# A decoder layer on one core: in the slots of the self attention, scores by keys are issued ahead of scores by queries

## The chip, the cores and the metric

The kernel runs on one core of a Trainium2 chip. Its engines are TensorE (PE in the profile, with PEld for its weight loads), VectorE (DVE), ScalarE (ACT), GpSimd (POOL) and SyncE (SP, which here only issues DMA transfers). The metric is the device time of one execution in microseconds (us). Before the change the median of three runs is 703.72 us (701.57 to 704.51).

## The reference

One decoder layer on x of shape (4, 1024, 256), four batches, in float32:

```
x = x + self_attention(layernorm(x))            # windows of 128, 16 heads of 16
x = x + cross_attention(layernorm(x), context)  # 77 keys, a mask, projections with biases
x = x + ffn(layernorm(x))                       # fake-quantised, silu(gate) * up, 704 wide
```

In the self attention a query of chunk c sees the keys of chunk c-1 and, causally, those of its own chunk c:

```
scores = einsum('bhcqd,bhckd->bhcqk', qc, kcat) / HD ** 0.5
scores = where(causal & valid, scores, -inf)
out    = einsum('bhcqk,bhckd->bhcqd', softmax(scores), vcat) @ w_out
```

## The kernel before, in words

The attention phase is a software pipeline written out by hand: the order of the instructions on each engine is the order in which the Python code issues them. Its work is cut into jobs, self attention (S) or cross attention (X) of one batch, in the order S0, S1, S2, X0, S3, X1, X2, X3. A job is cut into groups (g, o) of four heads, and a group into units u: four units of two 128-row tiles for S, two units of four tiles for X. That makes 96 units, and one slot of the main loop (line 1120) for each, after some slots ahead of the first.

Scores are computed twice. By queries (`sc_n`, `maxima`, line 616, products at L627) they stand with queries on the partitions, and VectorE takes each row's maximum from them (L657, with the causal mask `cboth` added); by keys (`sc_t`, `weights`, line 701, products at L712) they stand with keys on the partitions, and ScalarE takes the exponentials (L722), GpSimd zeroes what is not causal (L726). For the second kind, the negated maxima must already stand in `q`: each head has 16 spare rows there, and one of them, against a row of ones in `k`, adds the maximum's negative to every product. `put_maxima` (line 676) brings them there: a transpose on TensorE (`ps_mx`, L679), a copy on ScalarE (`mxT`, L683) and four DMA transfers issued by SyncE (L686). So `sc_t` of a group's first unit waits for these transfers, and `sc_n` of a unit runs LEAD = 5 slots ahead of its `sc_t`.

In slot number `slot` the loop handles `now`, the unit of this number, and `ahead`, the unit five later. A slot issues in this order: weighted values (`ps_av`, L756) with their transpose on VectorE (L780) and the normalising (L788, L790, L802) for units two slots back, in every second slot; tasks chosen by due times and costs, which are projections (`project`, L583, emptied by ScalarE), values (`values`, L564, emptied by ScalarE), transposes of normed rows (`normed_T`, L544), output projections (`out_project`, L811, added to x by VectorE at L820), and preparation of weights, mask and cross keys; work beside them on VectorE (statistics at L189, quantising of the FFN's weights at L426 to L436); `put_maxima` if a group is complete; then the block that the change touches, the scores of `ahead` and of `now`.

All products of this phase go to one pool of eight PSUM banks (`ps_b`, line 204), handed out in the order of the program. A tile waits until the tile eight places earlier has been read to the end. A slot takes four banks for `sc_n`, four for `sc_t`, and one or two for each task. `max_bias` and `weight_bias` only take the banks for S units; for X units they also issue a product with the mask.

[...]

Of the kernel before, what the change touches and what calls it, by code (L numbers as in the profile page):

```python
# [24 lines left out]
def decoder_layer(  # L25
# [33 lines left out]
    B, S, D = x.shape  # L59
# [139 lines left out]
    with ExitStack() as att:  # L199
# [6 lines left out]
        def bank(name):  # L206
            return ps_b.tile([P, 512], F32, name=name, tag="b")
# [393 lines left out]
        def max_bias(job, g, o, u):  # L601

            if u == 0:
                job.mx[g, o] = work.tile([P, NJ, NT], F32, name="mx", tag="mx", bufs=3)
            job.nb = banks = [bank("sc_n") for _ in range(NJ)]
            for j in range(NJ):
                if job.kind == "X":
                    nc.tensor.matmul(  # L608
                        banks[j][:, : HT * SK],
                        ident_bf,  # L610
                        mb_n[:, u * HT : (u + 1) * HT, :].rearrange("p t k -> p (t k)"),
                        start=True,
                        stop=False,
                    )
# [61 lines left out]
        def put_maxima(job, g, o):  # L676

            ps = bank("ps_mx")
            nc.tensor.transpose(  # L679
                ps[: NJ * NT, :P], job.mx[g, o].rearrange("p j t -> p (j t)"), ident  # L680
            )
            mxT = work.tile([NJ * NT, P], F32, name="mxT", tag="mxT", bufs=2)
            nc.scalar.copy(mxT, ps[: NJ * NT, :P])  # L683
            for j in range(NJ):
                row = j * SL + (1 - o) * HD
                nc.sync.dma_start(  # L686
                    out=job.q[g, o][row : row + 1, :],
                    in_=mxT[j * NT : (j + 1) * NT, :],
                )

        def weight_bias(job, g, o, u):

            job.tb = banks = [bank("sc_t") for _ in range(NJ)]
            if job.kind == "X":
                s = slice(u * HS, (u + 1) * HS)
                for j in range(NJ):
                    nc.tensor.matmul(  # L697
                        banks[j][:SK], ident_bf[:SK, :SK], mb_t[:, s], start=True, stop=False
                    )

        def weights(job, g, o, u):

            q, banks = job.q[g, o], job.tb
            if job.kind == "S":
                k = job.k[g, o]
                w = 0
                for i in range(2):
                    t = 2 * u + i
                    n = min(2 * P, S - t * P)
                    for j in range(NJ):  # L710
                        r = slice(j * SL, (j + 1) * SL)
                        nc.tensor.matmul(  # L712
                            banks[j][:, w : w + n],
                            k[r, t * P : (t + 1) * P],
                            q[r, t * P : t * P + n],
                            start=True,
                            stop=True,
                        )
                    w += n
                for j in range(NJ):  # L720
                    pt = work.tile([P, 2, 2, P], F32, name="pt", tag="pt", bufs=16)
                    nc.scalar.activation(  # L722
                        pt.rearrange("p i a q -> p (i a q)")[:, :w], banks[j][:, :w], AF.Exp
                    )

                    nc.gpsimd.affine_select(  # L726
                        out=pt[:, :, 0, :],
                        in_=pt[:, :, 0, :],
                        compare_op=ALU.is_ge,
                        fill=0.0,  # L730
                        base=0,
                        pattern=[[0, 2], [1, P]],
                        channel_multiplier=-1,
                    )
                    job.pts[g, o, j, u] = pt
            else:
                k = kx[:, g, o, job.b * SK : (job.b + 1) * SK]
                s = slice(u * HS, (u + 1) * HS)
                for j in range(NJ):
                    r = slice(j * SL, (j + 1) * SL)  # L740
                    nc.tensor.matmul(banks[j][:SK], k[r, :], q[r, s], start=False, stop=True)  # L741
                for j in range(NJ):
                    pt = work.tile([SK, HS], F32, name="ptx", tag="pt", bufs=16)
                    nc.scalar.activation(pt, banks[j][:SK], AF.Exp)  # L744
                    job.pts[g, o, j, u] = pt
# [36 lines left out]
        def normalise(job, g, o, hf, tail):  # L782

            if o == 0:
                job.aN[g, hf] = work.tile([P, HS], F32, name="aN", tag="aN", bufs=2)
            on = job.av[g, o, hf].rearrange("p (s e) -> p s e", e=SL)
            rec = small.tile([P, HS // SL, 1], F32, name="rec")
            nc.vector.reciprocal(rec, on[:, :, HD : HD + 1])  # L788
            aN = job.aN[g, hf].rearrange("p (s e) -> p s e", e=SL)
            (nc.gpsimd if tail else nc.vector).tensor_tensor(  # L790
                aN[:, :, o * HD : (o + 1) * HD],
                on[:, :, 0:HD],
                rec.to_broadcast([P, HS // SL, HD]),
                ALU.mult,
            )

        def by_features(job, g, o, hf):

            if o == NS - 1:
                if g == 0:  # L800
                    job.aT[hf] = work.tile([P, NC, HS], F32, name="aT", tag="aT", bufs=3)
                nc.vector.transpose(job.aT[hf][:, g, :], job.aN[g, hf])  # L802
# [317 lines left out]
        for slot in range(first, last):  # L1120
            present["slot"] = slot
            now = units[slot] if 0 <= slot < N else None
            ahead = units[slot + LEAD] if 0 <= slot + LEAD < N else None
            for fn, args in early.get(slot, ()):
                fn(*args)
            tail = slot >= N - LEAD
            if slot == N:

                pair = values_of[slot] + values_of.pop(slot + 1)
                for args in pair:  # L1130
                    weighted_values(*args)
                    normalise(*args, tail)
                for args in pair:
                    by_features(*args)
                while beside:
                    t = min(beside, key=lambda t: t[1:3])
                    beside.remove(t)
                    t[4](*t[5])
                    while after:
                        after.pop(0)()  # L1140
                last_project(jobs[-1])
            else:
                for args in values_of.get(slot, ()):
                    weighted_values(*args)
                    normalise(*args, tail)
                    if not tail:
                        by_features(*args)
            spent = 0.0
            cap = 1.35 if now and ahead else 2.3
            while t := next_in(tasks, slot, spent, cap):  # L1150
                spent += t[3]
                fn, args = t[4:]
                fn(*args)
                if fn is out_project:
                    job, hf, t2 = args
                    if job.kind == "X" and t2 == HT // 2 - 1:
                        third_norm(job.b, hf, slot)
            spent = 0.0
            while t := next_in(beside, slot, spent, 1.2):
                spent += t[3]  # L1160
                t[4](*t[5])
            if tail and slot < N:
                for args in values_of.get(slot, ()):
                    by_features(*args)
            for args in puts.get(slot, ()):
                put_maxima(*args)
            if ahead:
                max_bias(*ahead)
                if now and now[0].kind == "X":
                    weight_bias(*now)  # L1170
                maxima(*ahead)
            if now:
                if not (ahead and now[0].kind == "X"):
                    weight_bias(*now)
                weights(*now)
            for fn, args in late.get(slot, ()):
                fn(*args)
            while after:
                after.pop(0)()
# [6 lines left out]
    with ExitStack() as ffn:  # L1186
# [237 lines left out]
        ahead = []  # L1424
# [57 lines left out]
```

## Time and profile before

| what | value |
|---|---|
| median of three runs | 703.72 us |
| the profiled execution, its own time | 704.22 us |
| its span | 702.5 us |
| mean granted TensorE clock | 0.99 |
| TensorE busy | 654.3 us (93%) |
| VectorE busy | 546.7 us (78%) |
| ScalarE busy | 367.5 us (52%) |
| GpSimd busy | 268.5 us (38%) |
| first `sc_t` of slot 0 | 38.8 us |
| slots 0 to 42 (`now` and `ahead` both S) | 36.4 to about 269 us |
| slots 56 to 66 (both S again) | 349.9 to about 407 us |

A profile row of the kind "L657 DVE ... x512 | 172.7, 403 | 39.4 <-PE sc_n L627 38.9" gives the line, engine and operation, the count, the busy time, the mean duration in ns, and behind the last bar the idle time of that engine just before these instructions with what ended most of it. Ends of matmuls are modelled, so a busy TensorE is not a TensorE at its peak. In a row of waits the numbers are the total in us, the count and the longest.

### The profile page before, as it was taken

To read this page: it belongs to the slowest core of one execution; us is meant where nothing else is said; L and a number is where in the kernel's file an instruction comes from. 1 tells how busy PE (TensorE), PEld (TensorE's weight loads), DVE (VectorE), ACT (ScalarE), POOL (GpSimd) and SP (SyncE) were. 2 spreads that over 40 slices of the span, in tenths; PEclk is the share of its full clock that TensorE was granted. 3 is DMA by queue.
4 is the path that set the end of the run, shared out by engine and by line. 5 is a ranking of instruction groups with operands and counts; after the bars stand their busy time and mean duration, and the time that the engine had idled before them with its cause. 6 is when DMAs were issued, how large, how long until landed. Compare 5 with 4: busy or idle time off the path is not lost.

```text
span 702.5 us, 17376 instructions
## 1 busy us (share of the span) xinstructions
PE 654.3 (93%) x6465; PEld 404.3 (58%) x6470; DVE 546.7 (78%) x1917; ACT 367.5 (52%) x672; POOL 268.5 (38%) x517
## 2 busy tenths in 40 slices
PE   8989999999999889999999999999999999778776
PEld 5566566667665666655567666544554537334555
DVE  5688769669787798667879977766766868789987
ACT  3545555534656436534464465345445475498393
POOL 4055524536236386700064787234411024111022
PEclk9999999999999999999999999999999999999999
DMA  8000100000000000000000000000000000000048
GB/s 291 9 3 11 35 3 18 2 19 19 24 4 9 10 10 11 20 2 17 3 9 25 26 24 24 3 2 4 17 17 3 18 17 16 0 2 0 1 67 174
DMA packets 18645, 17.02 MB, mean 24 GB/s; under 512 B 3788, under 2 KB 18049, under 8 KB 18561
## 3 DMA queue, kind: packets, MB, share of 16 engines
q1 hardware_dynamic: 16369, 14.08, 6.4%
q0 software_dynamic: 1904, 1.84, 2.1%
q8 instruction: 51, 0.84, 0.5%
q14 instruction: 33, 0.27, 0.1%
q10 hardware_dynamic: 288, 0.00, 0.0%
HBM read 9.35 MB, written 6.03 MB: 22 GB/s over the span
## 4 chain that ended last, share of the span: by engine, by line
PE 70%; DVE 17%; ACT 6%; issue 4%; DMA 1%; POOL 1%; SPq 0%; ACTq 0%; DVEq 0%
PE ps_p L583 12%; PE sc_n L627 8%; PE ps_av L756 8%; PE sc_t L712 8%; PE ps_op L811 7%; PE sc_n L642 4%; PE ps_av L766 4%; PE sc_t L741 3%; PE ps_v L564 3%; PE sc_t L697 3%; DVE junk L657 2%; PE ps_t L544 2%; DVE bnst L189 2%; PE sc_n L608 2%; DVE hq L1391 1%
## 5 line engine op out<-in xcount | busy, mean ns | idle before, releaser
L657 DVE CUSTOM_DVE_ANT_0 junk<-sc_n,cboth 128x256 bf16<-128x256 f32 (+1 forms) x512 | 172.7, 403 | 39.4 <-PE sc_n L627 38.9
L722 ACT ACTIVATE pt<-sc_t 128x512 f32<-128x512 f32 (+1 forms) x256 | 125.4, 576 | 99.1 <-PE sc_t L712 96.6
L726 POOL TENSOR_SCALAR_AFFINE_SELECT pt<-pt 128x256 f32<-128x256 f32 x256 | 102.3, 408 | 117.4 <-ACT pt L722 107.2
L744 ACT ACTIVATE ptx<-sc_t 77x512 f32<-77x512 f32 x128 | 65.5, 592 | 77.3 <-PE sc_t L741 77.3
L712 PE MATMUL sc_t<-q,k 32*128 32x256 f32 (+1 forms) x1024 | 87.9, 380 | 2.8 <-DMA q<-mxT 1.4
L668 DVE TENSOR_REDUCE mx<-sc_n 128x4 f32<-128x308 f32 x128 | 52.2, 470 | 37.0 <-PE sc_n L642 36.9
L627 PE MATMUL sc_n<-k,q 32*128 32x256 f32 (+1 forms) x1024 | 79.7, 391 | 0.7 <-DVE mx L657 0.7
L157 POOL TENSOR_SCALAR ve<-mv 128x4 f32<-128x4 f32 x20 | 4.6, 232 | 196.9 <-DVE mv L191 196.8
L712 PEld LDWEIGHTS sc_t<-q,k 32*128 32x128 f32 x1024 | 66.8, 188 | 13.4 <-ACT q L597 2.3
L529 POOL TENSOR_SCALAR xn<-x,mv,rs 128x256 f32<-128x256 f32 x56 | 70.2, 1260 | 0.0
L627 PEld LDWEIGHTS sc_n<-k,q 32*128 32x128 f32 x1024 | 49.6, 185 | 30.0 <-DVE mx L657 10.7
L583 PE MATMUL ps_p<-xnT,w_s 128*128 128x512 f32 x128 | 61.8, 611 | 2.5 <-DVE mx L657 1.1
L780 DVE STREAM_TRANSPOSE o_sb<-ps_av 128x512 f32<-128x512 f32 x63 | 45.0, 714 | 23.6 <-PE ps_av L756 14.4
L756 PE MATMUL ps_av<-pt,vt 128*32 128x256 f32 (+1 forms) x1152 | 59.2, 349 | 2.4 <-DVE mx L657 2.3
L756 PEld LDWEIGHTS ps_av<-pt,vt 128*32 128x32 f32 x1152 | 34.8, 110 | 30.7 <-DVE mx L657 6.0
L657 DVE DVE_READ_ACCUMULATOR2_ANT mx<- 128x1 f32 x512 | 42.6, 83 | 0.0
L642 PEld LDWEIGHTS sc_n<-kx,q 32*128 32x128 f32 x1024 | 31.5, 186 | 14.5 <-issue 14.5
L697 PE MATMUL sc_t<-mb_t,ident_bf 77*77 77x512 bf16 x128 | 35.3, 379 | 4.0 <-ACT q L593 3.6
L583 PEld LDWEIGHTS ps_p<-xnT,w_s 128*128 128x128 f32 x128 | 22.2, 189 | 28.1 <-issue 17.1
L642 PE MATMUL sc_n<-kx,q 32*128 32x77 f32 x1024 | 36.2, 277 | 0.0
L766 PE MATMUL ps_av<-ptx,vx 77*32 77x512 f32 x256 | 35.2, 604 | 0.6 <-DVE mx L668 0.6
L1304 DVE SCALAR_TENSOR_TENSOR hT<-pu,usc,act 128x512 f32<-128x512 f32 x44 | 30.6, 744 | 6.4 <-ACT act L1303 6.1
(204 smaller groups left out, 1097.7 us busy)
## 6 DMA issues: line engine op xcount, KB each, us to landing
x<-in_x_dram SPq DMA_DIRECT2D x8, 512.0 KB
out_dram<-y SPq DMA_DIRECT2D x9, 256.0 KB
q<-mxT SPq DMA_DIRECT2D x128, 4.0 KB
out_dram<-x SPq DMA_DIRECT2D x7, 256.0 KB
out_dram<-y POOLq DMA_DIRECT2D x7, 256.0 KB, 4.7
w_s<-in_L_attn_w_qkv_dram SPq DMA_DIRECT2D x2, 384.0 KB
raw_d<-in_L_ffn_w_down_dram SPq DMA_DIRECT2D x2, 352.0 KB
raw_f<-in_L_ffn_w_gate_dram SPq DMA_DIRECT2D x5, 128.0 KB
```

Of the source, the lines that this page charges most:

```text
L529: eng.tensor_scalar(xn, xb[job.b][:, t, :], job.st[hf].mv[:, i, 0:1], job.st[hf].rs[:, i : i + 1], ALU.subtract, ALU.mult,)
L583: nc.tensor.matmul(ps, w[:, c, g * P : (g + 1) * P], job.xnT[hf][:, c, :], start=(c == 0), stop=(c == NC - 1),)
L627: nc.tensor.matmul(banks[j][:, (i + 1) * 2 * P - n : (i + 1) * 2 * P], q[r, t * P : (t + 1) * P], k[r, k0 * P : k0 * P + n], start=True, s ...
L642: nc.tensor.matmul(banks[j][:, i * SK : (i + 1) * SK], q[r, t * P : (t + 1) * P], k[r, :], start=False, stop=(i == HT - 1),)
L657: nc.vector.tensor_tensor_reduce(out=junk[:, 2 * P - n :], in0=banks[j][:, (i + 1) * 2 * P - n : (i + 1) * 2 * P], in1=cboth[:, 2 * P - n ...
L697: nc.tensor.matmul(banks[j][:SK], ident_bf[:SK, :SK], mb_t[:, s], start=True, stop=False)
L712: nc.tensor.matmul(banks[j][:, w : w + n], k[r, t * P : (t + 1) * P], q[r, t * P : t * P + n], start=True, stop=True,)
L722: nc.scalar.activation(pt.rearrange("p i a q -> p (i a q)")[:, :w], banks[j][:, :w], AF.Exp)
L726: nc.gpsimd.affine_select(out=pt[:, :, 0, :], in_=pt[:, :, 0, :], compare_op=ALU.is_ge, fill=0.0, base=0, pattern=[[0, 2], [1, P]], channe ...
L744: nc.scalar.activation(pt, banks[j][:SK], AF.Exp)
L756: nc.tensor.matmul(ps[j * SL : (j + 1) * SL, (a0 - t0) * P : (a1 - t0) * P], slot_of(job.vs[kb // 2][:, kb % 2], heads[j]), job.pts[g, o, ...
L766: nc.tensor.matmul(ps[j * SL : (j + 1) * SL, :], slot_of(vx[:, job.b], heads[j]), job.pts[g, o, j, hf], start=True, stop=True,)
```

## The change

In slots where both `ahead` and `now` exist and both are of the self attention, the scores by keys of `now` are issued first, then the scores by queries of `ahead`. All other slots keep the old order: with no `ahead` or no `now`, with one of them of the cross attention, and the slots that have both of the cross attention.

```
             for args in puts.get(slot, ()):
                 put_maxima(*args)
+            if ahead and now and ahead[0].kind == now[0].kind == "S":
+
+                weight_bias(*now)
+                weights(*now)
+                max_bias(*ahead)
+                maxima(*ahead)
+                ahead = now = None
             if ahead:
                 max_bias(*ahead)
                 if now and now[0].kind == "X":
                     weight_bias(*now)
                 maxima(*ahead)
             if now:
                 if not (ahead and now[0].kind == "X"):
                     weight_bias(*now)
                 weights(*now)
```

No line below the inserted ones changes; the numbers of the lines behind them rise by seven.

More of the change, by code (lines that the diff above doesn't have):

```diff
@@ L1166, in decoder_layer @@
                 put_maxima(*args)
+            if ahead and now and ahead[0].kind == now[0].kind == "S":
+                weight_bias(*now)
+                weights(*now)
+                max_bias(*ahead)
+                maxima(*ahead)
+                ahead = now = None
             if ahead:
```

## The prediction

> **What bounds the kernel now.** I read the page first, then busy time by stretch, then the chain of waits and the waits of single engines in the stretches that the change touches.
>
> From the page (parts 1, 4 and 5):
>
> ```profile
> PE 654.3 (93%) x6465; PEld 404.3 (58%) x6470; DVE 546.7 (78%) x1917; ACT 367.5 (52%) x672; POOL 268.5 (38%) x517
> ...
> PE 70%; DVE 17%; ACT 6%; issue 4%; DMA 1%; POOL 1%; SPq 0%; ACTq 0%; DVEq 0%
> ...
> L657 DVE CUSTOM_DVE_ANT_0 junk<-sc_n,cboth 128x256 bf16<-128x256 f32 (+1 forms) x512 | 172.7, 403 | 39.4 <-PE sc_n L627 38.9
> L722 ACT ACTIVATE pt<-sc_t 128x512 f32<-128x512 f32 (+1 forms) x256 | 125.4, 576 | 99.1 <-PE sc_t L712 96.6
> ```
>
> TensorE holds 70% of the chain, VectorE 17%. ScalarE waited 96.6 us for `sc_t`: scores by keys that come earlier only let ScalarE wait elsewhere. VectorE waited 38.9 us for `sc_n`, over 64 self-attention units: 0.6 us each, so it has little room for scores that come later.
>
> The busy time of two stretches with an output projection in nearly every slot (the first and second rows), and TensorE's waits from slot 0 to slot 42:
>
> ```profile
> 240.60:261.40 20.80, 18.21 (x233) 13.44 (x230) 19.31 (x92) 8.67 (x18) 16.75 (x32) 1.00 0.03 9
> 379.30:399.10 19.80, 17.93 (x231) 13.78 (x230) 18.95 (x91) 8.68 (x18) 15.62 (x29) 1.00 0.11 35
> ...
> PE ps_av L756 <- DVE mx L657: 1.6, 3, 1.1
> PE sc_t L712 <- DMA q<-mxT: 1.4, 1, 1.4
> PE ps_p L583 <- DVE mx L657: 1.1, 1, 1.1
> PE ps_op L811 <- DVE mx L657: 1.0, 3, 0.4
> ```
>
> Columns of the first two lines: stretch, its us, busy TensorE, weight loads, VectorE (19.31 of 20.80 and 18.95 of 19.80), ScalarE, GpSimd, granted clock, DMA. There VectorE is the bound and TensorE waits for it; elsewhere in the touched slots TensorE runs almost without a gap.
>
> **The change part by part.** It adds and removes no instruction. In slots 0 to 42 and 56 to 66, 54 of them, TensorE's two blocks change places: eight `sc_t` products (`now`) ahead of eight `sc_n` products (`ahead`). The order within VectorE, ScalarE, GpSimd and each DMA queue stays, so no transfer is moved past another. What moves besides is the ring of eight PSUM banks, handed out in program order. With e banks taken by a slot's tasks, the ring was: tasks take the first e banks of the last `sc_n`, `sc_n` the rest of them and some of the last `sc_t`, and `sc_t` ends on the banks of this slot's own tasks. Now tasks take banks of the last `sc_t` (freed by ScalarE), `sc_t` ends on the first e banks of the last `sc_n`, and `sc_n` ends on the banks of this slot's own tasks.
>
> Slot 16 as it stands now, from the instructions in order of time (TensorE, then the DMA queue):
>
> ```profile
> 116.86 1.98 PE L583 MATMUL ps_p<-xnT,w_s 128*128 128x512 f32 x4
> 118.78 1.15 PE L627 MATMUL sc_n<-k,q 32*128 32x256 f32 x16
> 119.75 1.58 PE L712 MATMUL sc_t<-q,k 32*128 32x256 f32 x16
> ```
> ```profile
> 115.87 2.82 SPq L686 DMA_DIRECT2D q<-mxT  x4
> ```
>
> `sc_n` takes 0.97 us to the start of `sc_t`; an `sc_t` that waits for nothing takes 1.04 (105.25 to 106.29); here it took 1.58 since its last bank was the projection's and ScalarE emptied that until 120.15.
>
> *B, the maxima's transfer.* The first `sc_t` of a group of four units reads rows of `q` that four transfers write. The last landed at 119.83 (the trace's landing events), `sc_t` began at 119.75. In the new order it wants to begin at 118.78, where `sc_n` stood, and `sc_n` is queued behind it, then every later matmul. Landing of the fourth row less the old start of `sc_n`, for the groups at 57, 98, 119, 168, 191, 210, 233 and 373 us: 1.16, 0.66, 1.05, 0.66, 1.18, 1.03, 2.86, 0.97, sum 9.6; at 41 us it is part A, and in the other groups of the touched slots it is 0.1 or less. What `sc_t` lost there to its own waits (its block less 1.04, no more than the new wait) goes: 0.39, 0.66, 0.54, 0.54, 0.73, 0.54, 2.08, 0.19, sum 5.7. Net +3.9 us. Bounds: 0 if later waits for VectorE absorb it, 9.6 if the old stalls come back at `sc_n`, whose last bank is now the projection's. I take 3.9, since both stalls run at the same time.
>
> *A, the start.* In slot 0 `sc_n` of unit 5 ran at 37.3 to 38.2 while `sc_t` waited for its rows until 40.95; VectorE began its maxima at 40.48. Now those products come behind `sc_t`, about 41.3, plus 1.1 to the first maximum: 42.4, so 1.9 us late. VectorE idles 1.10 and 0.80 us in the next two slots, which can absorb all of it: 0 to 1.9, I take 1.0, the middle.
>
> *C, slots whose tasks VectorE empties.* `out_project` ends in an addition on VectorE (L820, 0.69 us), queued behind the last slot's maxima (eight times 0.345). The bank of that product was wanted by `sc_t`; now `sc_n` wants it, and the next maxima wait for `sc_n`. So VectorE finishes the addition and then idles while the blocked products run: by the nearest rows, slots 1 and 2 where `sc_n` was bank-bound, 1.10 and 0.80; with nothing blocked 1.16 from the first product to the first maximum (118.78 to 119.94). I take 0.9. In the two VectorE-bound stretches there are eight such slots: 7.2 us, less the idle time that VectorE has there now (20.80 - 19.31 + 19.80 - 18.95 = 2.3): +4.9. Seven more slots like them (four projections of the second job, `kx`, the mask, `wq_x`) lie where the chain is on TensorE alone: 0 to 6.3, I take 0, for VectorE has room. Ends for C: 0, if later operations of VectorE (statistics, quantising) fill the idle time, and 11.
>
> *D, the gain.* Tasks no longer wait for maxima: TensorE's idle time of that kind is 6.3 us over both regions (`ps_av` 1.6 and 0.7, `ps_op` 1.0 and 1.2, `ps_p` 1.1, `ps_f` 0.5, `ps_w` 0.2). Of it 4.4 lie in the VectorE-bound stretches, where an earlier TensorE only waits at `sc_n` instead; 1.9 are real. D = -1.9, ends 0 and -6.3.
>
> Slots whose tasks ScalarE empties (`ps_p`, `ps_v`) cost nothing: the same wait, 0.2 to 0.7 us, passes from `sc_t` to `sc_n`. What hides it is VectorE's idle time of 0.5 to 0.7 us in front of the maxima there (120 and 126 us); without that cover it is up to 0.7 in some 20 slots. Weighted values need exponentials two slots old and do not wait for them either way.
>
> Sum: 1.0 + 3.9 + 4.9 - 1.9 = +7.9 us on the profiled execution's 704.22 us (span 702.5 and 1.7 around it), which lies 0.5 above the median of the runs, 703.72. On the median: 711.6.
>
> [...] The trace shows the granted clock at 0.87 in 36.4 to 50 us and at 0.79 in 64 to 72, where matmuls of 256 columns went out every 0.43 us instead of 0.216; no single wait in front was over 1.2 us. [...]
>
> **The rivals.**
> 1. *Faster.* VectorE reaches the tasks' banks in time and D counts in full. Place: the end of `sc_n` in the projection slots. It decides if the last addition is over within about 1.0 us after the tasks, while `sc_t` runs: now the additions ended at 158.84, 246.29 and 257.14, all within 0.9 us of the tasks' end, which speaks for it; against it, additions at 164.80 and 252.41 ended 1.0 us after, and maxima now begin later. Then -6.3, and B partly hidden at +1: 698.4.
> 2. *No change.* Both engines' loops (maxima, next `sc_n`, next maxima) are as long as before; B is absorbed and A is nothing: C +2 less D 1.9: about 703.8. For it: the loop itself has no new part where ScalarE empties the tasks.
> 3. *Slower by more.* Later `sc_n` make VectorE late everywhere, and the delay of one slot reaches the next: A 1.9, B 9.6, C 4.9, D 0 and one more half-clock piece 1.7: 18.1 up, 721.8. For it: VectorE's busy share, 93 and 96% in the two stretches. Against: 38.9 us of VectorE's idle time.
>
> That the change does nothing is no rival: the order is written out by hand and no planner undoes it.
>
> **How the numbers follow.** The forecast (706 to 717) has 0.55, rival 1 0.14, rival 2 0.17, rival 3 0.14. The time is that of the forecast, 711.6. The range, 700.5 to 721.0, leaves out half of rival 1 and most of rival 3. A measurement of this kernel tells about 0.5% (3.5 us) from no change: faster 0.14, same 0.16, slower 0.70, since a small part of rival 2 and all of the forecast and rival 3 lie beyond it or near.
>
> **What would show it.** In the changed kernel's profile: `sc_t` waiting for the DMA of `mxT` with 8 to 11 us in all, not 1.4 (B); tasks no longer waiting for `mx` (D); VectorE's wait for `sc_n` (L657) up from 38.9 to 45 or more; VectorE's busy time unchanged, and its idle time in the stretch of the third job's projections up by 2 us or more (C); the first half-clock piece as before or longer; nothing changed after the last self-attention slot but a shift. I am wrong if the waits at `sc_n` stay below what the tasks gave up, or if the transfers' wait only replaces waits for VectorE that stood there anyway.

## The result, and the profile after

The changed kernel takes 712.12 us (median of 4 runs, 710.57 to 712.72) against 703.39 us for the kernel before on the same chip (701.57 to 704.51): a ratio of 1.0123, 95% interval 1.0096 to 1.015. It is slower by 8.7 us; the prediction said 711.6. The profiled execution took 711.96 us (span 710.2, granted clock 0.988), 7.74 more than the one of before. Line numbers behind L1166 are seven higher; the lines named below L1166 have not moved.

The page of the changed kernel, the same lines as before:

```profile
PE 664.2 (94%) x6465; PEld 407.7 (57%) x6470; DVE 545.2 (77%) x1917; ACT 366.5 (52%) x672; POOL 265.2 (37%) x517
...
PE 70%; DVE 16%; ACT 6%; issue 5%; DMA 1%; POOL 1%; SPq 0%; ACTq 0%; DVEq 0%
...
L657 DVE CUSTOM_DVE_ANT_0 junk<-sc_n,cboth 128x256 bf16<-128x256 f32 (+1 forms) x512 | 173.1, 403 | 62.7 <-PE sc_n L627 62.0
L722 ACT ACTIVATE pt<-sc_t 128x512 f32<-128x512 f32 (+1 forms) x256 | 125.2, 577 | 64.6 <-PE sc_t L712 64.5
```

Look at the last number of the two lower rows. ScalarE waits 32 us less for `sc_t` (96.6 to 64.5), VectorE 23 us more for `sc_n` (38.9 to 62.0). VectorE's work is what it was. TensorE's busy time is 9.9 us longer with the same instructions: a block whose products come out one by one counts as busy nearly throughout (2.33 of 2.39 us in slot 16, shown below), and products at half clock last longer (629 ns in place of 374 in slot 0 of the kernel before).

TensorE's waits from slot 0 to slot 42 (total, times, longest):

```profile
PE ps_mx L679 <- DVE mx L657: 2.7, 2, 1.7
PE sc_t L712 <- DMA q<-mxT: 1.4, 1, 1.4
PE sc_n L627 <- DVE x L820: 1.0, 2, 0.5
PE sc_n L627 <- DVE kx L358: 0.5, 2, 0.3
PE sc_n L627 <- ACT q L597: 0.3, 2, 0.2
```

No task waits for maxima (`mx`) any more, neither `ps_av` nor `ps_p` nor `ps_op`. What waits now is `sc_n`, for the bank of a task, and the transpose `ps_mx`.

The two stretches that the prediction called VectorE-bound, between the same instructions as before (stretch, its us, then busy TensorE, weight loads, VectorE, ScalarE, GpSimd, clock, DMA):

```profile
248.10:267.40 19.30, 18.63 (x233) 13.38 (x232) 18.25 (x85) 8.67 (x18) 15.63 (x30) 1.00 0.04 10
387.20:406.40 19.20, 18.75 (x231) 13.97 (x231) 18.45 (x87) 8.68 (x18) 15.62 (x30) 1.00 0.11 36
```

They got shorter, not longer: 19.3 us where it was 20.8, and 19.2 where it was 19.8, with VectorE idle for 1.05 and 0.75 us instead of 1.49 and 0.85. Part of it is only put off: VectorE has 7 and 4 instructions fewer inside them.

**Where the time came from.** Both orders issue the same score products, so the end of a slot (the last score product of that slot) can be compared between two executions. The difference to the kernel before is the *shift*; its growth from one slot to the next is what a slot costs. Most slots cost 0.00, and the rest few values, which come back in other kernels to a few hundredths. This is worked out from the traces (us; a blank is 0.05 or less):

| slots | changed | e3, old order in first units | e4, one transfer | e7 | e9 | e10 |
|---|---|---|---|---|---|---|
| 4 (first unit) | 0.86 | | -0.38 | | | |
| 5 | 0.46 | | 0.84 | | | |
| 6 to 8 (8 first unit) | -1.45 | -1.92 | -1.91 | -1.91 | -1.91 | -1.10 |
| 10 | 0.85 | 0.84 | 0.84 | | | 0.85 |
| 14 | 0.86 | 0.87 | 0.86 | 0.86 | | 0.87 |
| 16 (first unit) | 0.60 | -0.12 | -0.12 | -0.12 | -0.12 | |
| 21 | -0.39 | | -0.39 | | | |
| 22 | 0.28 | 0.28 | 0.28 | | | 0.28 |
| 23 | 0.54 | 0.54 | 0.54 | 0.81 | | 0.54 |
| 25 | 0.53 | 0.59 | 0.53 | 0.58 | | 0.58 |
| 28 (first unit) | 0.53 | | | | | |
| 30 | 0.65 | 0.65 | 0.65 | 0.66 | 0.65 | |
| 32 (first unit) | 0.58 | -0.12 | -0.12 | -0.12 | -0.12 | 0.68 |
| 36 (first unit) | -0.89 | -1.75 | -2.10 | -1.75 | -1.75 | -0.36 |
| 37 to 43 (first stretch) | -0.79 | 0.39 | -0.80 | 0.40 | 0.39 | |
| 60 (first unit) | 1.22 | 0.23 | -0.29 | 0.23 | 0.39 | |
| 61 to 67 (second stretch) | -0.09 | 0.39 | 0.15 | 0.39 | 0.39 | |

Two things in it come from the profiled execution of before and not from the change. In slot 36 that execution waited for a late transfer: the last piece of the fourth landed 2.85 us after the slot's first score product. The run with the new order in slots 0 to 3 alone (e11), whose slot 36 is as before, has 1.10 there and the same -1.75. The late landing is no single accident, for e2, e5 and e10 have it too (2.4 to 2.7 us, steps of -0.44, -0.14 and -0.36); why four of the ten traces with four transfers have it is open. And the execution of before ran at half clock from 67 to 71 us, where most others did not (-1.1 in slots 6 to 8 in kernels whose slots 6 to 8 are as before).

### The profile page after: what moved, and what is told of

Same layout as the page of the kernel before. It is cut to its first block, busy times and chain, and to the rows that moved or that the text cites. A ratio compares the mean times of both kernels' runs of the same rounds, so it can differ in the third digit from the quotient of the medians.

```text
span 710.2 us, 17386 instructions
## 1 busy us (share of the span) xinstructions
PE 664.2 (94%) x6465; PEld 407.7 (57%) x6470; DVE 545.2 (77%) x1917; ACT 366.5 (52%) x672; POOL 265.2 (37%) x517
## 4 chain that ended last, share of the span: by engine, by line
PE 70%; DVE 16%; ACT 6%; issue 5%; DMA 1%; POOL 1%; SPq 0%; ACTq 0%; DVEq 0%
PE ps_p L583 12%; PE sc_n L627 10%; PE sc_t L712 9%; PE ps_op L811 6%; PE ps_av L756 6%; PE sc_n L642 4%; PE ps_av L766 4%; PE sc_t L741 3%; PE ps_v L564 3%; DVE junk L657 3%; PE sc_t L697 3%; PE ps_t L544 2%; PE sc_n L608 2%; DVE hq L1398 1%; DVE hT L1311 1%
## 5 line engine op out<-in xcount | busy, mean ns | idle before, releaser
L722 ACT ACTIVATE pt<-sc_t 128x512 f32<-128x512 f32 (+1 forms) x256 | 125.2, 577 | 64.6 <-PE sc_t L712 64.5
L627 PE MATMUL sc_n<-k,q 32*128 32x256 f32 (+1 forms) x1024 | 95.8, 385 | 2.6 <-DVE x L820 1.4
L627 PEld LDWEIGHTS sc_n<-k,q 32*128 32x128 f32 x1024 | 66.0, 188 | 19.9 <-DVE mx L657 4.6
L712 PEld LDWEIGHTS sc_t<-q,k 32*128 32x128 f32 x1024 | 58.0, 187 | 30.4 <-issue 17.6
L599 ACT ACTIVATE k<-ps_p,onerow,rows 128x512 f32<-128x512 f32 x32 | 23.1, 773 | 28.1 <-PE ps_p L583 28.1
L593 ACT ACTIVATE q<-ps_p,bq_p,qrows 128x512 f32<-128x512 f32 x32 | 23.1, 775 | 26.8 <-PE ps_p L583 26.8
```

What stands on the lines that cost most here:

```text
L627: nc.tensor.matmul(banks[j][:, (i + 1) * 2 * P - n : (i + 1) * 2 * P], q[r, t * P : (t + 1) * P], k[r, k0 * P : k0 * P + n], start=True, s ...
L712: nc.tensor.matmul(banks[j][:, w : w + n], k[r, t * P : (t + 1) * P], q[r, t * P : t * P + n], start=True, stop=True,)
L722: nc.scalar.activation(pt.rearrange("p i a q -> p (i a q)")[:, :w], banks[j][:, :w], AF.Exp)
```

## The experiments

All were compared with the kernel before on the same chip. In the order of the changed block, `now` gives `sc_t` and `ahead` gives `sc_n`.

**e1 and e2: the order or the banks?** The change moves two things, the products' order and the order in which the PSUM banks are taken. e1 has the new issue order with the old ring of banks, e2 the old issue order with the new ring:

```
e1: max_bias(*ahead); weight_bias(*now); weights(*now); maxima(*ahead)
e2: weight_bias(*now); max_bias(*ahead); maxima(*ahead); weights(*now)
```

> The new issue order with the old ring of banks (all four banks of the scores by queries are handed out first, then the four of the scores by keys, but the products by keys are issued first). Theory (the loss comes from the order: the scores by keys come to the maxima's rows too early, and at the start the scores by queries come too late): most of the loss stays, 709 to 712 us. Rival (the loss comes from the ring, since the scores by queries end on the banks of the slot's own tasks): back to 703 to 705 us.

> The old issue order with the new ring of banks. Theory (order): 702 to 705 us, perhaps below the kernel before by the 2 to 6 us that tasks no longer wait for maxima. Rival (ring): 708 us or more.

e1: 710.49 us, ratio 1.0093 (1.0072 to 1.0114). e2: 704.67 us, ratio 1.0003 (0.9985 to 1.0021). The order makes the loss; the ring by itself neither costs nor gains that could be measured. In e1's trace the shift has the same steps as in the changed kernel (0.86 in slot 4, 0.84 in 10, 0.86 in 14, 0.59 in 16 and so on), and from slot 0 to the end of the attention it grows by 6.5 us, against 6.7, so the ring adds next to nothing to the new order either.

**e3: without the first units.** The old order stays where `now` is the first unit of a group, the one whose `sc_t` needs the transfers:

```
-            if ahead and now and ahead[0].kind == now[0].kind == "S":
+            if ahead and now and ahead[0].kind == now[0].kind == "S" and now[3]:
```

> The change in all its slots but those whose scores by keys are of a group's first unit, the only ones that read freshly transferred maxima. Theory (part B, the wait for the rows): the wait of scores by keys for the transfer is as before, and 5 to 7 of the 8.7 us go (start included, since slot 0 is a first unit): 705 to 707 us. Rival (scores by queries one block later are what costs, in every slot alike): three quarters of the loss stay, 710 us.

707.63 us, ratio 1.004 (1.0022 to 1.0059). So the first units hold some two thirds of the loss and not all of it. The table shows which part went: the steps in slots 4, 16, 28, 32, 36 and 60 (and 0.46 in slot 8), together 5.1 us. The steps in slots 10, 14, 22, 23, 25 and 30 stayed. The start is regained in part (slot 0 is a first unit), and the two stretches lose 0.39 us each instead of gaining.

**e4 and e6: one transfer instead of four.** If `sc_t` of the first unit waits for the last of four transfers, one transfer that lands sooner must take the wait away, with the new order left in place. e4 is the changed kernel with this edit, e6 the kernel before with it:

```
-            for j in range(NJ):
-                row = j * SL + (1 - o) * HD
-                nc.sync.dma_start(
-                    out=job.q[g, o][row : row + 1, :],
-                    in_=mxT[j * NT : (j + 1) * NT, :],
-                )
+            nc.sync.dma_start(out=job.q[g, o][(1 - o) * HD :: SL, :], in_=mxT)
```

> The changed kernel with the maxima's four transfers made into one of the same bytes (four rows, every 32nd partition). The last row then lands about 2.2 us earlier (three issues of 0.73 us fewer). Theory (part B and the start are waits for the last row): the scores by keys no longer wait for it, 704 to 706 us, or less if tasks then run ahead. Rival (the rows are not what counts, the maxima come late because of the order): 710 us or more.

> The order of before, with the four transfers of a group's maxima made one: the control of the run with the new order and one transfer. In the kernel before the scores by queries waited 1.4 us for these transfers where they stood behind the scores by keys, so at most 1.5 us are to be had: 702.0 to 703.7. If the earlier landing were worth as much here as with the new order (7 us), 696 to 697, and the wait for the transfers would not be what the new order lost.

e4: 704.96 us, ratio 1.0021 (1.0 to 1.0041): 1.0 of the 1.23% is gone. About 1 us of that may be the clock, for e4's executions had a mean granted clock of 0.990 and those of before 0.986 (under e12 it is said what such a difference is worth). e6: 701.97 us, ratio 1.0 (0.998 to 1.0019); its median is 1.3 us below that of before, as expected, but the interval does not tell it from nothing. So the earlier landing is worth some 6 to 7 us with the new order and about 1, not told from nothing, with the old one: the new order made TensorE depend on it. In slot 16 of the changed kernel, from the timeline (start, us, engine, line; first the queue of SyncE, then TensorE):

```profile
121.02 2.82 SPq L686 DMA_DIRECT2D q<-mxT  x4
```
```profile
121.89 1.98 PE L583 MATMUL ps_p<-xnT,w_s 128*128 128x512 f32 x4
123.81 2.19 PE L712 MATMUL sc_t<-q,k 32*128 32x256 f32 x15
125.66 0.39 PE L627 MATMUL sc_n<-k,q 32*128 32x256 f32 x3
```

and the same place in e4 (its lines behind the edit are five lower):

```profile
119.89 0.54 SPq L684 DMA_DIRECT2D q<-mxT  x1
```
```profile
120.76 1.98 PE L583 MATMUL ps_p<-xnT,w_s 128*128 128x512 f32 x4
122.68 1.15 PE L707 MATMUL sc_t<-q,k 32*128 32x256 f32 x16
123.64 1.58 PE L627 MATMUL sc_n<-k,q 32*128 32x256 f32 x16
```

Issuing four transfers takes 2.82 us, one takes 0.54. With four, `sc_t` needs 2.19 us for 15 of its 16 products, which all take 1.15 in e4, and `sc_n` starts 1.85 us behind it instead of 0.96. The wait does not stand in the list of waits, because `sc_t` had started: only some of its products need the last row, and the block stretches. By the trace's landing events the four transfers land at 122.79, 123.52, 124.26 and 124.98, and `sc_n` starts 0.68 us after the last landing, in this slot as in slots 4, 8, 12, 28, 32, 36 and 60. The issues begin 0.72 to 0.73 us apart and the landings come 0.72 to 0.74 us apart, so what the runs show as the reason is the time to issue.

**e5: the new order in projection slots alone.** It was meant for term C. The edit takes the new order where an `out_project` was among the slot's tasks. That was twelve slots, not the eight that the expectation names: 37 to 40 and 61 to 64, and also 21, 22, 23 and 25 of the second job.

```
+            projected = False
             spent = 0.0
...
                 if fn is out_project:
+                    projected = True
...
-            if ahead and now and ahead[0].kind == now[0].kind == "S":
+            if ahead and now and ahead[0].kind == now[0].kind == "S" and projected:
```

> The new order only in the eight self-attention slots in which an output projection is issued; all other slots keep the order of before. The prediction's term C (VectorE waits for the product of scores by keys, 4.9 us over the eight slots of the two stretches): 5 us slower, about 708.5. The rival, read from the shift between the two traces after the change (+0.1 at the start of the stretch of 240 to 261 us to -1.4 at its end, with the tasks freed from the maxima): the stretch gains 1 to 3 us, 700.8 to 702.7. Between them (703 to 706) the gain seen there was only the making up of delays that earlier slots had caused.

704.01 us, ratio 1.0016 (1.0002 to 1.003). The total is between the two expectations since it is a sum of both signs: the shift falls by 0.71 in slots 37 to 43 and by 0.27 in 61 to 67, and grows by 0.28, 0.54 and 0.58 in slots 22, 23 and 25. C, a loss in the two stretches, is refuted; the gain there is 1.0 us, at the low end of what the rival said. It hangs on slots 40 and 64 being new as well: in e3, e7 and e9, which keep the old order in them as first units, the same stretches cost 0.4 us each.

**e7: and without the preparation slots.** e3's remaining steps lie where weights, keys and mask for the cross attention are prepared. e7 is e3 with the old order also in the slots that issue such a task (9, 12, 14, 18, 20, 21, 25, 27 and 30):

```
+                if t[3] == 0.3 and fn.__name__ in ("turn", "context", "keys", "<lambda>", "mask_T"):
+                    prepared = True
...
-            if ahead and now and ahead[0].kind == now[0].kind == "S":
+            if ahead and now and ahead[0].kind == now[0].kind == "S" and now[3] and not prepared:
```

> The new order in all self-attention slots but the first units of a group (which wait for the transfers) and the slots in which a preparation for the second attention is issued as a task (keys, mask, weights turned). If those preparation slots are where the run without the first units still lost time (its shift grew by 0.9 at the keys, 1.1 at the mask, 0.7 at the weights and fell by 2 in the projection stretch): 703.4 to 705, no longer slower. If the order itself costs its 0.4% in all slots alike: 707 again.

706.76 us, ratio 1.0046 (1.0031 to 1.0061): nothing regained, the expectation missed. But the steps moved in a telling way. Slot 14 is back in the old order and still costs 0.86; slot 10 keeps the new order and costs nothing, now that slot 9 is old. What counts is the order of the slot *ahead* (for slot 25 it is slot 23, two ahead: 24 is old here and in e3 and e10).

**e8: a try at a faster kernel.** New order from slot 4 on, not in preparation slots, one transfer; the edits are those of e4 and e7 with `slot >= 4` in place of `now[3]`.

> The new order from the fifth slot on, not in the slots with a preparation for the second attention, with one transfer of a group's maxima instead of four. By the shift of the run with one transfer (start +2.4, preparations +2.5, projection stretches -3.5): without its two losses 699 to 702, faster than both kernels. If the losses of start and preparations only move on to the slots behind them: 703 to 705.

705.11 us, ratio 1.0025 (1.001 to 1.004). Missed, for the same reason as e7: slots 4, 13, 22, 23 and 29 are new, and slots 5, 14, 23, 25 and 30 cost 0.84, 0.86, 0.81, 0.53 and 0.65.

**e9 and e10: the slots ahead.** e9 has the new order in all slots but the first units and six slots ahead of a slot that costs; e10 in these six alone:

```
e9:  ... == "S" and now[3] and slot not in (9, 13, 21, 22, 23, 30):
e10: ... == "S" and slot in (9, 13, 21, 22, 23, 30):
```

The expectations contain two slips. The step of 0.65 belongs to slot 30, so the slot ahead of it is 29, which e9 leaves in the new order; and the touched slots are 54, not 56.

> The run before left the preparation slots themselves in the old order and lost 3.1 us of shift all the same, at slots 14, 23, 25 and 31, each time behind a slot in the new order. This one has the new order in all slots but the first units of a group and the slots ahead of those that pay: 9, 13, 21, 22, 23 and 30. Theory: the scores by keys come second there, VectorE's 2.85 us of reductions start about 1 us later, and what VectorE must empty for the next slot's tasks stands behind them. Then nothing is left of the 3.8 us: 703.4 to 704.8, and a shift that stays within 0.3 us from slot 4 to slot 35. The rival, that each change between the two orders costs by itself: 706 to 708.

> The complement: the new order in slots 9, 13, 21, 22, 23 and 30 alone, six of the 56. Theory, from the steps of the shift in the run without first units (0.85 at slot 10, 0.86 at 14, 0.28 at 22, 0.54 at 23, 0.59 at 25, 0.65 at 31): +3.8, 706.5 to 707.5. The rival, that the loss is spread over all slots that change: 0.6 us at most, 703.2 to 704.2.

e9: 704.51 us, ratio 1.0014 (0.9995 to 1.0033). From slot 9 to slot 29 its shift stays between -0.96 and -1.15; slots 10, 14, 22, 23 and 25 cost nothing, and slot 30 costs 0.65, as it must with slot 29 new. e10: 706.27 us, ratio 1.004 (1.0019 to 1.0061): six of 54 slots bring a third of the loss, with 0.85, 0.87, 0.28, 0.54 and 0.58 in slots 10, 14, 22, 23 and 25, none in slot 30, and 0.68 in slot 32, which was not expected. There slot 31, back in the old order, finds VectorE late by the work of slot 30, and the projection of slot 32 waits for a bank that slot 31's maxima have not yet read; the same product waits for nothing in the kernel before:

```profile
212.39 1.98 PE L583 MATMUL ps_p<-xnT,w_s 128*128 128x512 f32 x4 [0.73 <-DVE mx L657]
```

So VectorE's lateness can also come out one slot further on. For slot 14 all four combinations have been run:

| | slot 14 old | slot 14 new |
|---|---|---|
| slot 13 old | 0 (before) | 0.00 (e9) |
| slot 13 new | 0.86 (e7), 0.87 (e10) | 0.86 (changed), 0.87 (e3) |

The timelines show how. e9, slot 13 old:

```profile
105.31 2.34 PE L350 MATMUL ps_kx<-cT,wk_x 128*128 128x308 f32 x8
...
107.24 2.12 DVE L358 TENSOR_SCALAR kx<-ps_kx,rows,bk_p 128x308 f32<-128x308 f32 x4
107.58 1.15 PE L712 MATMUL sc_t<-q,k 32*128 32x256 f32 x16
108.55 0.60 PE L627 MATMUL sc_n<-k,q 32*128 32x256 f32 x6
109.41 1.12 PE L627 MATMUL sc_n<-k,q 32*128 32x256 f32 x10 [0.26 <-DVE kx L358]
```

e10, slot 13 new:

```profile
106.83 1.04 PE L627 MATMUL sc_n<-k,q 32*128 32x256 f32 x16
...
107.80 2.34 PE L350 MATMUL ps_kx<-cT,wk_x 128*128 128x308 f32 x8
107.89 0.42 DVE L657 CUSTOM_DVE_ANT_0 junk<-sc_n,cboth 128x256 bf16<-128x256 f32 x1 [2.35 <-PE sc_n L627]
...
110.65 2.11 DVE L358 TENSOR_SCALAR kx<-ps_kx,rows,bk_p 128x308 f32<-128x308 f32 x4
...
111.81 0.69 PE L712 MATMUL sc_t<-q,k 32*128 32x256 f32 x2 [0.17 <-DVE kx L358]
112.82 1.13 PE L712 MATMUL sc_t<-q,k 32*128 32x256 f32 x10 [0.32 <-DVE kx L358]
```

In the new order `sc_n` is the last thing ahead of the next slot's task. VectorE idles 2.35 us, starts its maxima as the task starts on TensorE, and comes to the task's banks (`kx`) 2.85 us after the task's first product instead of 1.93. The banks are free 0.92 us later and the scores that want them wait that much longer. In the changed kernel nothing of this is seen where ScalarE empties the slot's tasks (0.00 in slots 11, 15, 17 and 33 to 35, for example), nor where a `project` or `values` for ScalarE stands beside a task for VectorE: slots 9, 12, 18, 20, 26 and 27 cost 0.03 or less.

**e11: the start alone.** New order in slots 0 to 3:

```
+            if ahead and now and ahead[0].kind == now[0].kind == "S" and slot < 4:
```

> The new order in slots 0 to 3 alone. The prediction's term A gave this stretch +1.0: 704.4. The shift of the changed kernel (+1.08 ahead of slot 0, +3.54 behind slot 3) gives +2.4: 705.8, of which up to 1.7 could be one more stretch at half clock, which then would not be in every run.

704.93 us, ratio 1.0018 (0.9997 to 1.0039), between the two expectations. In its trace the shift grows by 2.15 from ahead of slot 0 to behind slot 2 (1.68 to 3.83), and by another 1.64 in slot 3, where this execution had a stretch at half clock. The size is thus 1.4 by the medians and 2.2 by the trace; the runs do not tell more closely.

**e12: a second try at a faster kernel.** One transfer, and the new order only in slots 37 to 40 and 61 to 64:

```
+            if ... == "S" and slot in (37, 38, 39, 40, 61, 62, 63, 64):
```

> One transfer of a group's maxima instead of four, and the new order only in the eight slots of the two stretches of the third and fifth job that issue output projections (37 to 40 and 61 to 64), where the shift fell in every run. Their share was -0.5 and -0.2 us in the run with these slots, -0.8 and -0.2 with one transfer; with the 1 us of one transfer by itself: 701.0 to 702.5. The rival, that the gain of the stretches is only the making up of earlier delays: 702.5 to 703.5, as with one transfer alone.

703.46 us, ratio 0.9999 (0.9979 to 1.0019): no gain that could be measured, as the rival had it. Yet the steps in its trace are those of a gain, -0.64 in slots 37 to 43 and -0.21 in 61 to 67. Its profiled execution had eight stretches at half clock instead of four; two views of it (third number from the end: the clock):

```profile
47.00:54.00 7.00, 7.00 (x54) 5.35 (x50) 5.50 (x32) 3.38 (x7) 4.80 (x9) 0.51 0.01 2
664.00:672.00 8.00, 5.91 (x40) 4.59 (x40) 5.37 (x13) 2.30 (x3) 0.00 (x0) 0.57 0.00 0
```

Its other executions had more of them too: over the twelve the mean granted clock is 0.984, over the 35 of before 0.987, so about 2.1 us more were lost at half clock (one less the clock, times the span). Within one kernel, executions took 0.5 us longer for each us so lost, over all runs with a clock on record, so that some 1 us of gain may be hidden in e12. That is an estimate from these numbers; a gain is not shown.

No kernel here was measurably faster than the kernel before.

## Why the prediction was right, and where it was not

The time was right to 0.5 us, the sign was right, and the account behind it was half right: two terms grew, one had the wrong sign, and a term that had been set to zero took its place. By the steps of the shift in the changed kernel:

| term | predicted | measured in the trace | shown by |
|---|---|---|---|
| A, start | +1.0 | +2.5 | e11: +1.4 to +2.2 |
| B, transfers | +3.9 | +5.1 | e3, e4 |
| C, eight slots of the stretches, with D there | +4.9 | -0.9 | e5 |
| C, other slots emptied by VectorE | 0 | +4.2 | e9, e10 |
| D, tasks freed from the maxima, elsewhere | -1.9 | -1.4 | trace only |
| sum | +7.9 | +9.5 | medians: +8.7 |

The measured terms are sums of steps: A is the shift behind slot 3, 3.54, less 1.08 ahead of slot 0. B is the changed kernel's step less e3's in the first units (0.86, 0.46, 0.72, 0.53, 0.70, 0.86 and 0.99 in slots 4, 8, 16, 28, 32, 36 and 60). The third line is the steps of the two stretches, -0.79 and -0.09. The fourth is 0.46, 0.85, 0.86, 0.28, 0.54, 0.53 and 0.65 in slots 5, 10, 14, 22, 23, 25 and 30. What is left goes to D: -0.39 in slot 21, -0.8 in slots 6 to 8 (the change there beyond before's own half-clock stretch), and a few between -0.12 and 0.23. The profiled pair differs by 7.7 and not by 9.5, for before's execution had lost 2.85 us of its own (1.75 and 1.1, above), and the changed kernel's lost 1.1 ahead of slot 0, with a stretch at half clock from 10 to 14 us. That the profiled difference equals the predicted +7.9 is thus partly luck. The time itself is so near by luck too: A and B together came 2.7 us above their sizes, and C, over all its slots, 1.6 below.

*A, the start: right in mechanism, too small.* The prediction had VectorE's maxima of slot 0 late by 1.9 us, half absorbed. They came 3.6 us late (40.48 in the kernel before to 45.12 in the changed one, less the shift of 1.08):

```profile
40.48 0.39 DVE L657 CUSTOM_DVE_ANT_0 junk<-sc_n,cboth 128x256 bf16<-128x256 f32 x1
45.12 0.42 DVE L657 CUSTOM_DVE_ANT_0 junk<-sc_n,cboth 128x256 bf16<-128x256 f32 x1 [3.47 <-PE sc_n L627]
```

The delayed products ran at half clock. This is the first half-clock piece, which the prediction wanted "as before or longer"; it is twice as long, in the view of busy time by stretch:

```profile
41.00:48.00 7.00, 6.86 (x52) 5.93 (x50) 3.49 (x20) 3.24 (x7) 4.10 (x12) 0.52 0.01 3
```

The second half of that cost little, for e1, with one piece of 3.4 us there, grew by 2.4 us in the same slots. Only 1.1 of the 3.6 were absorbed. The second piece, at 67 us, is gone in exchange, so the clock cost the touched slots as much as before, which is what the prediction's sum had: 3.4 us in either trace, summed over windows of 1 us. The 1.7 us that rival 3 adds for one more piece is what a piece loses in these traces (1.71 at 67 us in the kernel before), but in the touched slots the changed kernel has none more. In the 20 us ahead of its piece at 41 us TensorE's longest wait was 1.4 us (`sc_t` for the transfers); what brings such a piece on is not shown.

*B, the transfers: right, by places too.* Predicted net per group against measured: 0.77 and 0.86 (slot 4), 0 and 0.02 (12), 0.51 and 0.72 (16), 0.12 and 0 (24), 0.45 and 0.53 (28), 0.49 and 0.70 (32), 0.78 and 0.86 (36), 0.78 and 0.99 (60). The group of slot 8, which the prediction set to 0.1 or less, cost 0.46. The failing detail is the sign by which it was to be seen: "8 to 11 us in all" in the waits. The list has 1.4 in slots 0 to 42, all of it in slot 0 and so part of A, and 0.7 in slot 60, since the wait hides in lengthened blocks.

*C: the step that failed.* "So VectorE finishes the addition and then idles while the blocked products run" took VectorE's queue to hold nothing but maxima and additions. The bound of the term said what could go wrong, "0, if later operations of VectorE (statistics, quantising) fill the idle time", and that end held: in the stretches VectorE's idle time fell, 1.49 to 1.05 and 0.85 to 0.75. The seven other slots, which the prediction set to 0 "for VectorE has room", were the opposite: VectorE has room there in the mean, but not in the 1 us that decides. Its lateness comes from the slot ahead, whose `sc_n` now stands last, and the price is 0.3 to 0.9 in seven slots. Four of them (14, 22, 23, 25) were on the prediction's list, for another reason; 5 and 10, with the transposes of `normed_T` that VectorE empties too, and 30, where `wo_x` is turned, were not.

*D: right in sign, and near in size as far as the rest tells.* No task of slots 0 to 42 waits for the maxima any more. Of the 6.3 us, 1.9 were counted; what the other terms leave over of the steps is 1.4 outside the stretches; no run tests it by itself. A new wait stands in its place, `ps_mx` for the maxima, 2.7 us where the kernel with the old order behind slot 3 (e11) has 1.3; in slot 7 it costs 1.0, and slot 8 gives 1.1 back.

*The rivals.* No change fell with A and B, 7.6 us together, which nothing made up for. Faster fell with them too: the gain that rival 1 saw in the projection slots is real, but 1 us in all (e5). Rival 3, that VectorE's delay reaches the next slot everywhere, was right about the way and wrong about "everywhere": in the changed kernel it does so in seven slots that have tasks for VectorE and none of `project` or `values`, which ScalarE empties.

*Right besides:* VectorE's wait for `sc_n`, predicted at 45 or more, is 62.0, and behind the last touched slot nothing but a constant shift is seen (7.78 there and 7.76 at the end of the attention).

## What to carry to other kernels

When two products on one in-order engine change places, ask who consumes the one that now comes last, and what stands behind that consumer's work in its own queue when the next slot begins: here VectorE's maxima moved 0.9 us closer to the next task and held up that task's banks, in slots that looked free by their busy share. A product that needs a transfer must not stand ahead of one that needs none, unless the transfer has landed: one place in the queue made 5 us of it here. And the shift of the same instruction between two traces, slot by slot, tells more than the sums of waits, where these 5 us stand with 0.7.

## What the runs showed of the hardware that was not expected

In these fourteen traces the stretches at half clock (a granted clock of 0.50) are of one length: each loses 1.70 or 1.71 us (the sum of one less the clock over windows of 1 us), and the long ones, with 3.41 or 3.42, are two in a row. The profiled executions have from three (e1, e7) to eight (e12) of them, before four, the changed kernel five, at varying places: at 10 to 17 us, 40 to 57, 67 to 75, and two to four from 600 us on, in the feed-forward part that no experiment touched. A kernel whose steps add up to a gain of 1 or 2 us can so come out even, as e12 may have done. Whether TensorE's waits bring more of them is open: e1, one of the slowest, has three, and e12 and e6 have eight and six, but e7 has three too. The mean clock over all executions of a kernel does not settle it: 0.990 for e1 and for e4, 0.988 for e7, 0.986 for e6 and 0.984 for e12.

Issuing the four transfers of 4 KB from SyncE took 2.82 us and one strided transfer of the same 16 KB took 0.54, which with this order of products was worth 1% of the kernel, and with the other nothing that could be measured.
